# A graph layer and an expert layer in one kernel: the ranking of each group's expert choices is put a slot earlier, and its sums, places and sends with it

## The chip, the cores and the metric

The kernel runs on one NeuronCore of a Trainium2 chip. The metric is the time on the device in microseconds (us), the median of several runs. The core's engines each work through a queue of their own in order and wait for each other through semaphores: TensorE (PE; its weight loads are shown as PEld), VectorE (DVE), ScalarE (ACT), GpSimd (POOL) and SyncE (SP), which here only issues transfers. POOL issues the indirect transfers (gathers and scatters of rows by index).

## What is computed

There are 6250 nodes with 256 features and 100000 edges with 96 features, sorted by the node that they end in. All is float32.

```python
xn   = layernorm(x)
sum_, max_, mean_ = per node over its edges: sum, max (0 if none), sum / max(count, 1)
h    = relu(concat[xn, sum_, max_, mean_, u[0]] @ W1 + b1) @ W2 + b2      # 1024 hidden
x1   = x + h + xn
g    = layernorm(x1)
v, e = top_k(g @ gate_w + gate_b, 2)                                      # 2 of 16 experts
w    = softmax(v)
y    = g + sum over the two: w_k * (relu(g @ w1[e_k] + b1[e_k]) @ w2[e_k] + b2[e_k])
out  = x1 + layernorm(y) * gamma + beta
```

## The kernel before

**Tiles and groups.** The nodes are 50 tiles of 125. Thirteen groups of four tiles (group 0 has two) are worked from the last nodes to the first. The edges' sums and maxima come from two sources: groups 0 and 1 gather windows of edges; for all others an "edge stream" on DVE runs over seven regions of the edges (regions 0 to 6), loads chunks (`raw`), makes running sums and maxima (`rw`, lines 323 to 327), and stores them to `rows_d` through SP (line 336). At the end of a region its run sums are joined over partitions (`chain_runs`, lines 382 to 446, with two small transposes on PE), and a "carry" is stored to `carry_d` on POOL's queue (line 444). Groups then gather rows (`take_edges`, line 726) and carries (`take_carry`, line 733), and DVE joins them (`join_edges`, lines 739 and 741).

**Slots.** The order of the work is written out by hand: `at_slot(T, fn, ...)` puts a function into slot T, twelve slots to a group, and the list is sorted by slot and then by the order of entry (lines 1354 to 1371). Emitted in that order, each instruction joins the queue of its engine. Group g's matmuls stand in slots 12g to 12g+11: eight of `hidden` (line 775) and four of `output` (line 783, one per tile). What follows group g stands among group g+1's matmuls. Counted from slot 12(g+1): 0, the last `residual` (line 788); 1 to 3, `root_b`, `scale_b` and `norm_b` (line 811, ACT), which writes the normed rows twice into `xr`; 4 and 5, `turn_b` (line 820, PE); 6, `logits` (line 828, PE); 7, `choose` (lines 835 to 842: DVE takes the two best of 16 per row, ACT an exponential); 8, `rank`; 9, `rank_2`; 10, `place`; 11 and the slot after it, `send`, two tiles each. `xr` has one buffer, so the next group's `norm_b` must wait until the sends have read it.

**Ranking and sending.** `rank` (lines 848 to 855, DVE) turns the choices into a mask `mm` and adds it to running counts `M`, tile by tile. `rank_2` (lines 862 and 863, PE) multiplies by a triangular matrix and by ones, which sums over partitions and gives every row its number within its expert; it writes the PSUM tile `pg`, of which there is one, also used by `logits` and `bounds`. `place` (lines 871 to 884, DVE) turns that into row addresses in `xg_d` and writes the weights and the return addresses into `xr`. `send` (line 888, POOL) scatters 125 rows of 1032 bytes for each of a tile's two choices, with a small memset after each (line 893).

**The planner's credit.** Between two slots the loop gives the edge stream what is left of 4.6 us after the slot's own costs (`cost=` in `at_slot`). So a step that is put elsewhere also moves stream items. Small PE steps of the stream are held back to a slot's end (`for_pe`, `tell_pe`).

**Gathers between.** `take_blocks` (line 499) gathers blocks of dst on POOL's queue, in slots that fall among the places and sends of groups 1, 3 and 4; it is entered after them in the list, so within one slot it stands after them.

**Experts.** After the groups, `xg_d` is worked in blocks of 256 rows: `load_block` (lines 1025 to 1032, SP: two register loads, the rows `xb`, the 1 MB weights `wt`, the bias `eb`), `turn_block` (lines 1039 to 1050) for the next block in the middle of a block, `run_block` (lines 1061 to 1085: two matmul layers, and the results scattered by POOL to `y_d`). A block's load is issued three blocks ahead. The load reads `xg_d` at an address from a register, so it waits for all sends that were emitted before it, and sends wait for loads emitted before them. Blocks 0 to 13 are placed at slot 156 + 1.6b, so the steps that follow the last group (group 12, from slot 156) lie among them: `choose` in slot 163 stands after block 4 (162.4), slot 164's steps before block 5 (164.0), and so on. A last phase adds the two results of each node, norms and writes.

Of the kernel before, what the change touches and what calls it, by code (L numbers as in the profile page):

```python
# [35 lines left out]
SLOTS = 12  # L36
# [7 lines left out]
def kernel(  # L44
# [1047 lines left out]
    def at_slot(T, fn, *a, cost=0.0):  # L1092
        tasks.append((T, len(tasks), fn, a, cost))
# [15 lines left out]
    for g, (a, z) in enumerate(GRP):  # L1109
        B, n = SLOTS * g, z - a  # L1110
# [4 lines left out]
    for g, (a, z) in enumerate(GRP):  # L1115
        B, n = SLOTS * g, z - a
        if g:
            if g > 1:
                at_slot(max(0, B - 17), take_x, g)
                at_slot(B - 14, stats_x, g, 0, cost=1.2)  # L1120
                at_slot(B - 13, stats_x, g, 1, cost=1.2)
            if g > 1:
                at_slot(B - 11, root_x, g)
                at_slot(B - 10, scale_x, g, cost=0.5)
            at_slot(B - 9, norm_x, g)
            for i in range(n):
                if g >= GW:
                    late = 3 if g == GW else 0
                    at_slot(B - 10 + late + i // 2, take_edges, region[g], g, i)
                    at_slot(B - 9 + late + i // 2, take_carry, region[g], g, i)  # L1130
                else:
                    for h in range(2):
                        at_slot(2 * i + h, cut_window, g, i, h * WE // 2, (h + 1) * WE // 2, None)
                        at_slot(2 * i + 1 + h, sum_half, g, i, h)
                    at_slot(2 * i + 1, max_window, g, i, cost=4.7)
                    at_slot(2 * i + 2, add_window, g, i, cost=0.9)
                    at_slot(2 * i + 2, mask_window, g, i, cost=0.4)
                    at_slot(min(2 * i + 5, SLOTS - 2), mean_window, g, i)
            at_slot(B - 7, keep_x, g)
            for k in range(DC):  # L1140
                at_slot(B - 6 + k, turn, g, k)
            for i in range(n if g >= GW else 0):
                at_slot(B - (4 if g == GW else 6) + i // 2, join_edges, g, i, cost=0.6)
                at_slot(B - (4 if g == GW else 5) + i // 2, mask_edges, g, i)
            for k in range(DC, KC + 1):
                at_slot(B - 3 + k - DC + (1 if g == GW and k < DC + 2 else 0), turn, g, k)
        for i in range(n):
            at_slot(B + HC + 1 + i, residual, g, i, cost=1.1)
        early = GS - n
        at_slot(B + SLOTS + 1 - early, root_b, g)  # L1150
        at_slot(B + SLOTS + 2 - early, scale_b, g, cost=0.3)
        at_slot(B + SLOTS + 3, norm_b, g)
        for k in range(DC):
            at_slot(B + SLOTS + 4 + k, turn_b, g, k)
        at_slot(B + SLOTS + 6, logits, g)
        at_slot(B + SLOTS + 7, choose, g, cost=2.2)
        at_slot(B + SLOTS + 8, rank, g, cost=1.3)
        at_slot(B + SLOTS + 9, rank_2, g)
        at_slot(B + SLOTS + 10, place, g, cost=1.5)
        for i in range(n):  # L1160
            at_slot(B + SLOTS + 11 + i // 2, send, g, i)
    T = SLOTS * (NG - 3) + 21
    at_slot(T, open_experts)
    at_slot(T, count_full)
# [137 lines left out]
    with tc.manual_schedule():  # L1302
# [54 lines left out]
        for slot, _, fn, args, cost in tasks:  # L1357
            while slot > T:
# [6 lines left out]
                g = min(T // SLOTS, NG - 1)  # L1365
# [123 lines left out]
```

## Time and profile before

| | us |
|---|---|
| median of 3 runs | 1401.33 (1400.38 to 1401.83) |
| profiled execution, its own time | 1403.48 |
| its span | 1401.7 |
| PE busy in the span | 1195.1 |
| DVE busy in the span | 898.2 |
| granted TensorE clock, mean | 0.932 |

The profile's page lists busy time per engine over the span and in 40 equal slices of 35 us (a digit is tenths). Groups of instructions are named by line, engine, operation and tiles, output before inputs; each row of the timeline has start, duration, engine, line, operation, tiles, count, and in brackets the idle time of the engine just before it and what ended that. The name of what ended a wait is inferred from semaphores and can be a neighbour's. On PE each float32 matmul shows as two records, so an `output` of 8 matmuls shows as 16.

The rows at the places that the change touches, by group (us from the span's start):

| group | choose | rank | rank_2 on PE, wait before it | place | sends |
|---|---|---|---|---|---|
| 1 | 250.4 | 253.0 | 258.4, 0 | 262.7 | 273.9 to 287.0 |
| 3 | 369.9 | 374.3 | 375.1, 4.1 | 382.0 | 393.6 to 406.8 |
| 4 | 436.7 | 441.1 | 443.9, 0 | 450.1 | 462.5 to 478.2 |
| 9 | 740.4 | 744.3 | 745.1, 2.9 | 749.5 | 751.5 to 763.1 |
| 11 | 836.0 | 837.8 | 846.1, 0 | 846.7 | 849.5 to 861.1 |
| 12 | 906.1 | 907.9 | 914.4, 0 | 923.0 | 926.5 to 944.5 |

### The profile page before, as it was taken

The numbers are of one execution on the slowest core, as the hardware profiler recorded it, in microseconds if no ns is written. First come the engines' busy times: TensorE is split into PE (matmuls) and PEld (weight loads), VectorE is DVE, ScalarE is ACT, GpSimd is POOL, SyncE is SP. The second block draws the span as 40 slices with busy tenths as digits, with TensorE's granted clock in tenths as the row PEclk, the third lists the DMA queues.
The fourth block names the chain that finished last, engine by engine and source line by source line (L and its number), as shares of the span: only waits on it lengthen the run. The fifth ranks groups of instructions, "written<-read, shape, count | busy, mean of one in ns | idle before, by whom it ended". The sixth has DMA issues, their size and how long they took to land. (4 is left out here: it accounts for less than half of the span.)

```text
span 1401.7 us, 16643 instructions
## 1 busy us (share of the span) xinstructions
PE 1195.1 (85%) x4835; PEld 833.7 (59%) x4835; DVE 898.2 (64%) x2319; ACT 510.6 (36%) x1178; POOL 519.4 (37%) x611
## 2 busy tenths in 40 slices
PE   2598458979869789998898998899999999999683
PEld 1263244636626364564545647787888888888562
DVE  5477669969986989998777314343444455444277
ACT  3485135644528354353343532211212212121233
POOL 4133044563374736346253414152333333333100
PEclk9898779989989899999999999999999999999897
DMA  6953687796979897898985143457667786766396
GB/s 163 205 139 103 167 247 189 223 264 180 266 203 254 242 275 202 241 267 221 262 244 167 33 158 120 170 176 253 228 232 268 246 271 223 240 216 208 104 273 194
DMA packets 187240, 292.28 MB, mean 209 GB/s; under 512 B 35309, under 2 KB 153582, under 8 KB 179840
## 3 DMA queue, kind: packets, MB, share of 16 engines
q1 hardware_dynamic: 150800, 234.36, 56.5%
q0 software_dynamic: 36224, 56.33, 14.3%
q8 instruction: 41, 0.67, 0.2%
q14 instruction: 63, 0.52, 0.1%
q10 hardware_dynamic: 112, 0.41, 0.1%
HBM read 169.70 MB, written 123.21 MB: 209 GB/s over the span
## 5 line engine op out<-in xcount | busy, mean ns | idle before, releaser
L775 PE MATMUL acc<-inT,w1x 128*128 128x500 f32 (+1 forms) x832 | 378.7, 606 | 0.0
L775 PEld LDWEIGHTS acc<-inT,w1x 128*128 128x128 f32 x832 | 164.1, 205 | 184.8 <-issue 182.5
L1080 POOL DMA_INDIRECT y_d<-yb,to_i x114 | 133.1, 1168 | 296.6 <-ACT yb L1079 272.9
L1061 PE MATMUL acc<-xT,wt 128*128 128x256 f32 x912 | 223.1, 388 | 8.0 <-ACT hb L1067 6.2
L1074 PE MATMUL acc<-wt,hb 128*128 128x256 f32 x912 | 207.7, 380 | 6.5 <-DVE hb L1065 6.5
L888 POOL DMA_INDIRECT xg_d<-xr,pos_i x100 | 127.8, 1278 | 206.0 <-DVE xr L884 127.3
L783 PE MATMUL acc<-w2s,hT 128*125 128x256 f32 x800 | 187.9, 392 | 12.9 <-ACT hT L777 12.9
L1061 PEld LDWEIGHTS acc<-xT,wt 128*128 128x128 f32 x912 | 169.4, 191 | 39.8 <-ACT hb L1067 15.5
L1074 PEld LDWEIGHTS acc<-wt,hb 128*128 128x128 f32 x912 | 172.5, 190 | 32.4 <-DVE hb L1065 8.9
L1079 ACT ACTIVATE yb<-yb,xb 128x256 f32<-128x256 f32 x114 | 51.8, 501 | 348.1 <-issue 300.6
L783 PEld LDWEIGHTS acc<-w2s,hT 128*125 128x125 f32 x800 | 153.5, 196 | 37.2 <-ACT hT L777 13.3
L777 ACT ACTIVATE hT<-acc,c 128x500 f32<-128x500 f32 (+1 forms) x104 | 68.4, 658 | 225.2 <-PE acc L775 224.9
L1077 DVE TENSOR_TENSOR yb<-acc,xb 128x512 f32<-128x512 f32 x57 | 39.4, 691 | 162.8 <-PE acc L1074 162.8
L499 POOL DMA_INDIRECT gb<-in_dst_dram,blk_i x50 | 69.0, 1381 | 117.2 <-DVE blk_i L496 52.0
L323 DVE TENSOR_TENSOR rw<-rw,keep 125x768 f32<-125x768 f32 x81 | 76.9, 949 | 46.5 <-DMA rows_d<-rw 46.5
L1041 DVE COPY xT<-pT 128x512 f32<-128x512 f32 x57 | 39.3, 690 | 77.8 <-PE pT L1039 73.2
L324 DVE TENSOR_TENSOR rw<-rw,bar 125x768 f32<-125x768 f32 x81 | 84.7, 1046 | 0.0
L327 DVE TENSOR_TENSOR rw<-rw,raw 125x768 f32<-125x768 f32 x88 | 83.8, 952 | 0.0
L326 DVE TENSOR_TENSOR rw<-rw,raw 125x768 f32<-125x768 f32 x88 | 83.6, 950 | 0.0
L726 POOL DMA_INDIRECT at<-rows_d,first_i x44 | 64.4, 1464 | 35.0 <-issue 25.4
L760 ACT COPY inT<-pT 128x500 f32<-128x500 f32 (+1 forms) x65 | 35.9, 552 | 88.5 <-PE pT L759 81.7
L1408 PE MATMUL py<-yk,ident 125*125 125x256 f32 x200 | 52.2, 419 | 18.4 <-DMA yk<-y_d 18.1
(288 smaller groups left out, 1516.4 us busy)
## 6 DMA issues: line engine op xcount, KB each, us to landing
wt<-in_wpack_dram SPq DMA_DIRECT2D x57, 1026.0 KB
rows_d<-rw SPq DMA_DIRECT2D x46, 960.0 KB
rows_d<-rw SPq DMA_DIRECT2D x46, 540.0 KB
raw<-in_edge_dram SPq DMA_DIRECT2D x46, 480.0 KB
xb<-xg_d SPq DMA_DIRECT2D x57, 258.0 KB
raw<-in_edge_dram SPq DMA_DIRECT2D x46, 270.0 KB
eb<-in_eb_dram SPq DMA_DIRECT2D x57, 128.0 KB
xt<-in_x_dram SPq DMA_DIRECT2D x12, 500.0 KB
```

What stands on the lines that cost most here:

```text
L323: nc.vector.tensor_tensor(su, prev[0], keep[c][:, :, s + j, None].to_broadcast(bcast), op=OP.mult)
L324: nc.vector.tensor_tensor(mx, prev[1], bar[c][:, :, s + j, None].to_broadcast(bcast), op=OP.min)
L326: nc.vector.tensor_tensor(su, su, x_j, op=OP.add)
L327: nc.vector.tensor_tensor(mx, mx, x_j, op=OP.max)
L499: nc.gpsimd.indirect_dma_start(out=gbs_[t], out_offset=None, in_=dst_b, in_offset=IndirectOffsetOnAxis(ap=blk_i[:, t:t + 1], axis=0))
L775: nc.tensor.matmul(pH[:, :n * P], w1x[:, k, ms], inT[:, k, :n * P], start=False, stop=(k == KC - 1))
L777: nc.scalar.activation(h[:, :n * P], pH[:, :n * P], AF.Relu, bias=c1[:, m:m + 1])
L783: nc.tensor.matmul(pO, G[g]["hT"][m][:, i * P:(i + 1) * P], w2s[:, m, :], start=(m == 0), stop=(m == HC - 1))
L888: d = nc.gpsimd.indirect_dma_start(out=xg_d[:, :], out_offset=IndirectOffsetOnAxis(ap=G[g]["pos"][:, i, k:k + 1], axis=0), in_=G[g]["xr"][ ...
L1061: nc.tensor.matmul(pB[i][:, half, :], wt[:, k * FF + m * 128:k * FF + (m + 1) * 128], xT[:, k, :], start=(k == 0), stop=(k == DC - 1))
L1074: nc.tensor.matmul(pY[:, h, :], hb[:, m, h * 128:(h + 1) * 128], wt[:, W2O + m * D:W2O + (m + 1) * D], start=(m == order[0]), stop=(m == o ...
L1080: d = nc.gpsimd.indirect_dma_start(out=y_d[:, :], out_offset=IndirectOffsetOnAxis(ap=BL[b]["to"][:, h:h + 1], axis=0), in_=yb[:, h, :], in ...
```

## The change

`rank` goes from slot 8 to slot 7, right behind `choose` of the same group; `rank_2`, `place` and the sends each go one slot earlier, in all thirteen groups. No instruction is added or removed; tiles, buffers and costs stay as they are.

```diff
         at_slot(B + SLOTS + 6, logits, g)
         at_slot(B + SLOTS + 7, choose, g, cost=2.2)
-        at_slot(B + SLOTS + 8, rank, g, cost=1.3)
-        at_slot(B + SLOTS + 9, rank_2, g)
-        at_slot(B + SLOTS + 10, place, g, cost=1.5)
+        at_slot(B + SLOTS + 7, rank, g, cost=1.3)
+        at_slot(B + SLOTS + 8, rank_2, g)
+        at_slot(B + SLOTS + 9, place, g, cost=1.5)
         for i in range(n):
-            at_slot(B + SLOTS + 11 + i // 2, send, g, i)
+            at_slot(B + SLOTS + 10 + i // 2, send, g, i)
```

In the queues this means: on PE, `rank_2` stands before the next group's second output and not after it (for group 12, before block 5 and not after it); on DVE, `rank` stands before the second pair of `join_edges`, and `place` before the first `residual`; on POOL, the first four sends of groups 1, 3 and 4 stand before a `take_blocks` and not after it, and for group 12 all eight sends stand before block 7 and before block 10's load, where four stood after both.

## The prediction

> **What bounds the kernel now.** I read the busy rows by slice first, then stretches of the span, then PE's waits, then the order of time around them.
>
> ```profile
> PE 1195.1 (85%) x4835; PEld 833.7 (59%) x4835; DVE 898.2 (64%) x2319; ACT 510.6 (36%) x1178; POOL 519.4 (37%) x611
> PE   2598458979869789998898998899999999999683
> DVE  5477669969986989998777314343444455444277
> DMA  6953687796979897898985143457667786766396
> ```
>
> A slice is 35 us. To about 745 us (slice 21) DVE and the DMA engines are as full as PE; from there to 1305 PE alone is. The stretches say the same:
>
> ```profile
> 255.00:275.00 20.00, 19.34 (x88) 13.71 (x87) 19.28 (x46) 11.20 (x33) 7.14 (x6) 1.00 0.59 168
> 275.00:300.00 25.00, 14.86 (x41) 6.17 (x40) 21.36 (x42) 9.63 (x19) 21.13 (x24) 0.85 0.92 244
> 420.00:745.00 325.00, 293.69 (x1062) 172.09 (x1062) 278.33 (x677) 148.88 (x314) 156.20 (x146) 0.93 0.88 246
> 750.00:890.00 140.00, 132.81 (x559) 89.66 (x558) 47.61 (x179) 47.04 (x85) 49.99 (x71) 1.00 0.37 117
> 960.00:1305.00 345.00, 343.01 (x1624) 292.26 (x1623) 156.02 (x327) 74.16 (x183) 115.62 (x181) 1.00 0.69 232
> ```
>
> Columns: stretch, its length, busy time of PE, its weight loads, DVE, ACT, POOL, then granted clock, DMA share, GB/s. Up to 745 us what decides is whichever of DVE and PE last waited for the other; after it every idle microsecond of PE counts in full.
>
> **Part 1: the sends leave POOL's queue sooner (groups 1, 3, 4).** In group 1 `place` ends at 264.4, yet its sends start at 273.9: four gathers of dst blocks (slot 34, L499) stand before them, and those wait until 267.2 for their indices.
>
> ```profile
> 267.22 1.24 POOL L499 DMA_INDIRECT gb<-in_dst_dram,blk_i  x1 [5.29 <-DVE blk_i L496]
> 273.94 1.43 POOL L888 DMA_INDIRECT xg_d<-xr,pos_i  x1 [0.30 <-issue]
> 285.56 1.43 POOL L888 DMA_INDIRECT xg_d<-xr,pos_i  x1 [0.21 <-issue]
> ```
>
> ```profile
> 295.75 2.93 ACT L811 ACTIVATE xr<-xt,stat 125x512 f32<-125x512 f32 x4 [12.46 <-DMA gb<-in_dst_dram,blk_i]
> ```
>
> ```profile
> 307.47 0.32 DVE L739 SCALAR_TENSOR_TENSOR at<-cg,cross,at 125x96 f32<-125x96 f32 x1 [8.88 <-DMA cg<-carry_d,next_i]
> ```
>
> `xr` has one buffer, so ACT's next norm waits for the last send to land (issued 285.6, landed about 295.6, though the row names a gather), and PE's turn at 296.6 waits 9.4 us with it; the carry gathers behind the sends hold DVE 8.9 us. After the change `place` follows the run sums directly and ends near 259.9; four sends fit between 260 and 266, before the gathers. Carry store 2 (0.6 us) moves behind the gathers, so the last four sends run 274.5 to 281.4 instead of ending at 287.0: **-5.6 us**, and the later gathers, ACT's norm and DVE's join come as much sooner. DVE reaches that join at 298.6, so 8.9 us of wait can give 5.6. Eight transfers and eight small memsets move; their count is unchanged. Here the Trainium skill speaks against the change: DMA: Bandwidth & Descriptors, section Issuing engines are not separate DMA queues, says that transfers from any engine share the same 16 engines, so an earlier issue buys no bandwidth. By the rule alone the gain is 0 if DMA limits; the row of 255 to 275 has DMA at 0.59, that is 8 us free, and four sends are about 0.5 MB, some 2 us at the 244 GB/s of the next row. I take -5.6 (bounds -6.5, 0). Groups 3 and 4 have the same queue (sends 393.6 to 406.8 behind gathers at 387.0; 462.5 to 478.2 behind 456.4), and PE waits for `xr` 12.8 and 4.9 us. But DVE stands at 429.7 for 13.3 us on a row store on SP's queue, not on `xr`, so a sooner PE only waits for DVE: 0 (bounds -8, 0, see the first rival).
>
> **Part 2: PE's sum over partitions (rank_2).** `rank` costs the same 1.6 us on DVE; it loses the join and stream work between it and `choose`. But rank_2 stands one output (3.6 us) sooner in PE's queue, and behind it wait output 1, the turns and the next group. In groups 3 to 9 PE already waits there:
>
> ```profile
> 735.14 7.07 PE L783 MATMUL acc<-w2s,hT 128*125 128x256 f32 x32
> 745.08 0.43 PE L862 MATMUL pg<-mm,before 125*125 125x64 f32 x2 [2.86 <-DVE mm L853]
> 747.00 5.09 PE L783 MATMUL acc<-w2s,hT 128*125 128x256 f32 x16
> ```
>
> In groups 3 to 8 (rank_2 from the end of `choose` + 1.9 us, then one output of 3.5 us) PE comes 0.1 to 2.9 us later, 4.6 in group 3 where the planner puts two more stream items ahead. DVE takes the residuals 2.6 to 12.8 us after PE has them, so this is hidden: 0 (bounds 0, +2); without that slack it is some 9 us. Group 0: +3.1, hidden by PE's wait of 5.1 us at 201.6. Group 9 is PE's last wait for DVE before the PE-bound part. `choose` ends at 742.2; unshifted, rank_2 ends 744.1 and the output 747.6 against 746.1, +1.5; by the planner's credit DVE has 1.9 us less ahead of it, -0.4. I take **+0.5** (bounds -0.4, +3). Groups 10 and 11: DVE waits for PE, sums are ready 5 us early: 0. The carry stores of regions 3 and 6 slip two slots and one: about 11 and 3.6 us on POOL, whose readers have that slack (joins at 365.5; DVE idle 7.7 us before 786.2): 0 (bounds 0, +4).
>
> **Part 3: the last group.** Slots are now expert blocks. Before, block 5 lay between `choose` and rank_2.
>
> ```profile
> 901.85 3.62 PE L1074 MATMUL acc<-wt,hb 128*128 128x256 f32 x16
> 905.31 1.89 PE L1061 MATMUL acc<-xT,wt 128*128 128x256 f32 x8
> 909.12 1.99 PE L1061 MATMUL acc<-xT,wt 128*128 128x256 f32 x8 [1.49 <-ACT hb L1067]
> ```
>
> After, rank_2 follows block 4 at once: PE idles from 905.5 to 908.7 (`mm` ends 908.67), rank_2 ends about 909.5, block 5 takes 7.6 and ends 917.1; block 6 began at 914.8 before: **+2.3 us**. The clock adds to it:
>
> ```profile
> 374.00:382.00 8.00, 6.88 (x22) 5.70 (x23) 7.73 (x17) 4.77 (x15) 0.00 (x0) 0.57 0.78 207
> 893.00:900.00 7.00, 7.00 (x26) 6.18 (x27) 0.00 (x0) 0.95 (x2) 1.48 (x4) 0.52 0.53 208
> ```
>
> The first followed a PE wait of 4.1 us, the second one of 1.7 us among small matmuls. The skill's TensorE: Matmul & The Clock Gate, section HAM oscillation, sets the limit at idle gaps of about 3.4 us: by it a gap of 3.2 costs nothing more; by the rows half clock follows for about 6 us, **+3.0** (bounds 0, +3.4). I take the rows.
>
> **Part 4: the last sends and the blocks' loads.** Before, four sends stood ahead of block 10's load and four ahead of block 11's; now all eight stand before block 10's, whose first transfer waits for them on SP with the weights and bias behind it.
>
> ```profile
> 943.28 1.18 POOL L888 DMA_INDIRECT xg_d<-xr,pos_i  x1 [0.21 <-issue]
> ```
>
> ```profile
> 947.45 0.31 SPq L1028 DMA_DIRECT2D xb<-xg_d  x1
> ```
>
> ```profile
> 955.04 0.69 DVE L1044 TENSOR_TENSOR xb<-xb,eb 128x512 f32<-128x512 f32 x1 [3.46 <-DMA eb<-in_eb_dram]
> ```
>
> The load goes 2.8 us after the last send ends; the bias lands 7.0 us after the weights are issued (948.0). The sends stay behind block 6's own scatters: 928.8 + 7 x 1.48 + 1.2 = 940.3, load at 943.5 (935.4 before), weights 944.1, bias 951.1. Block 9 then waits: DVE 951.1, PE 952.3, its end about 955.8 against 948.1. Block 10 no longer waits (2.8 us before) and ends 963.4 against 959.1: +4.3, of which 2.3 is part 3's: **+2.0**, and +1.5 for the clock over two PE waits of 4 and 3 us (bounds of both together 0, +7).
>
> **Sum.** -5.6 + 0 + 0.5 + 2.3 + 3.0 + 2.0 + 1.5 = **+3.7 us**. The profiled execution took 1403.48 us (span 1401.7 and 1.8 around it): 1407.2 there, span 1405.4; the runs' median lies 2.15 below it, so **1405.0 us** against 1401.33.
>
> **Rivals.** Faster: in group 3 the early sends fill the DMA hole of 388 to 394 us and are gone when SP comes to the row store that DVE then waits for. That store kept SP for 10.0 us (407.3 to 417.3), where the pieces beside it took 0.6 to 2.4; at 2 us DVE gains 8: 1405.0 - 8 = 1397.0. From 0.9 us on the kernel is not slower by the bound below, from 6.5 on it is faster. For it: DVE's 13.3 us wait at 429.7, DMA at 0.85 while those sends run. Against: the sends are only 4 of some 20 transfers on POOL's queue there. Clearly slower: the front gain is swallowed by the next row-store wait: 1405.0 + 5.6 = 1410.6; for it DMA at 0.88 from 420 to 745, against it nothing there is tied to a fixed time. Cancelled: no clock loss (-4.5): 1400.5.
>
> **How the numbers follow.** Forecast 0.50 (own range 1401 to 1409, a quarter of it inside the bound), faster rival 0.25, clearly slower 0.12, cancelled 0.13. A measurement of this kernel can tell 0.2%, 2.8 us: slower 0.38 + 0.12 + 0.01 = 0.51, same 0.12 + 0.10 = 0.22, faster 0.25 + 0.02 = 0.27. The range, 1393.5 to 1411, leaves about one in ten at each end.
>
> **What would show it.** Sends of group 1 on both sides of the four gathers; ACT's wait near 12.5 down to 7; DVE's wait for cg from 8.9 to 3; PE waiting about 3.2 us for mm between blocks 4 and 5, a half clock after it; the load of block 10 waiting for eight sends and block 9 standing on its bias. The prediction is wrong if DVE's later store waits change by more than some 5 us, or if the granted clock stays at 1.00 from 906 to 960.

## The result and the profile after

The changed kernel takes 1417.56 us (median of 4 runs, 1415.83 to 1419.93); the kernel before took 1400.86 us (1398.83 to 1401.83) beside it. The ratio is 1.0122, 95% interval 1.0103 to 1.0141: slower by 17 us, where 4 were predicted. The time lies outside the range of the prediction.

The busy rows of the page after, and its rows by slice:

```profile
PE 1204.4 (85%) x4835; PEld 837.6 (59%) x4835; DVE 901.4 (64%) x2319; ACT 512.1 (36%) x1178; POOL 533.3 (38%) x611
...
PE   2598459998898769898989998889999999999683
...
DVE  5477669986987789889887414343444444534277
...
DMA  5954676797879688988896243446677877766395
```

No engine has more instructions, and DVE has 3 us more of busy time in 14 us more of span. To see where the span grew I used `choose` (L835), which each group runs once on DVE, as a milestone:

| choose of group | before, us | after, us | difference |
|---|---|---|---|
| 0 | 188.3 | 187.7 | -0.6 |
| 1 | 250.4 | 254.1 | +3.7 |
| 2 | 311.9 | 308.9 | -3.0 |
| 3 | 369.9 | 380.1 | +10.2 |
| 4 | 436.7 | 441.7 | +5.0 |
| 6 | 568.8 | 577.1 | +8.3 |
| 9 | 740.4 | 750.2 | +9.8 |
| 12 | 906.1 | 913.1 | +7.0 |
| end of span | 1401.7 | 1415.8 | +14.1 |

So there are two losses. One builds up over the groups, with ups and downs: some 4 us by group 1, 10 by group 3 (where DVE has done one piece of edge work more than before: nine between choose of groups 2 and 3, not eight), 5 at group 4, and again nearly 10 at group 9; 7.0 are left at group 12. The other, 7.1 us, comes after the last `choose`. (Some of the expectations below split the 14.1 us as 9 and 5; the table gives 7.0 and 7.1.) Between choose of group 1 and of group 2 there is a gain of 6.7 us, at the place that part 1 of the prediction named.

**The first loss is idle time of DVE.** The stretch from choose of group 0 to choose of group 9 (columns as in the prediction: stretch, length, busy time of PE, its weight loads, DVE, ACT, POOL, then clock, DMA share, GB/s), before:

```profile
188.30:740.40 552.10, 484.11 (x1769) 286.19 (x1768) 476.39 (x1209) 253.26 (x546) 274.45 (x259) 0.92 0.85 236
```

and after:

```profile
187.70:750.20 562.50, 492.54 (x1759) 290.22 (x1760) 476.25 (x1206) 253.86 (x546) 286.20 (x259) 0.91 0.83 232
```

DVE does the same work, 476.4 and 476.25 us. The stretch is 10.4 us longer, and all of it is time in which DVE stands. What it stands for, in the view of its waits in that stretch (us in total, times, longest), before:

```profile
DVE rw L323 <- DMA rows_d<-rw: 34.8, 6, 13.3
DVE at L739 <- DMA cg<-carry_d,next_i: 12.6, 3, 8.9
DVE stat L803 <- ACT stat L798: 6.1, 4, 2.2
DVE bsa L690 <- DMA xt<-in_x_dram: 5.5, 6, 2.8
```

and after:

```profile
DVE bsa L690 <- DMA xt<-in_x_dram: 28.9, 7, 8.7
DVE at L739 <- DMA cg<-carry_d,next_i: 12.3, 6, 3.6
DVE rw L323 <- DMA rows_d<-rw: 9.2, 3, 3.3
DVE bsa L690 <- issue: 8.3, 1, 8.3
```

The waits for row stores did shrink, by 22 us with one of 3.3 that is put down to "issue". In their place DVE now stands 37.2 us (28.9 + 8.3) at L690, the first statistics of a group's x, because the load of x (`take_x`, L680, on SP's queue) has not landed. Before it was 5.5. The largest of these waits that the view puts down to the load, in the order of time after:

```profile
464.35 0.43 DVE L690 BATCH_NORM_STATS2 bsa<-xt 125x6 f32<-125x256 f32 x1 [8.65 <-DMA xt<-in_x_dram]
```

and SP's queue ahead of that load, after:

```profile
441.80 2.43 SPq L183 DMA_DIRECT2D raw<-in_edge_dram  x2
444.28 2.56 SPq L336 DMA_DIRECT2D rows_d<-rw  x2
446.95 1.71 SPq L680 DMA_DIRECT2D xt<-in_x_dram  x1
```

The same place before:

```profile
428.27 5.44 SPq L183 DMA_DIRECT2D raw<-in_edge_dram  x2
433.76 2.76 SPq L336 DMA_DIRECT2D rows_d<-rw  x2
436.61 1.85 SPq L680 DMA_DIRECT2D xt<-in_x_dram  x1
```

`take_x` of a group has the slot in which `choose` of the group three before it stands, so both can be measured from that choose. Over groups 3 to 11 before, SP issued the load 2.0 us after choose on average and DVE came to L690 15.6 us after choose. After, SP issues it 4.7 us after choose and DVE comes at 14.6. In the five groups in which DVE then waits more than 3 us, x takes 11 to 17 us from issue to use, 14 on average (the load is 500 KB). The 13.6 us that lay between before (15.6 - 2.0) held no slack; the 9.9 us after are 4 too few. In the program's order one piece of edge work more (a load and a row store) stands ahead of the loads of groups 6 and 7 on SP: 19 and 24 stores instead of 18 and 23. These two groups have 12.6 of the 37.2 us (4.0 and 8.7). For the other groups up to 11 SP's order is that of before: no piece passes their loads, but the same transfers are posted later after choose, or DVE comes to L690 sooner. In group 5, with the wait of 8.3 us, choose came 3.0 us sooner than before and the load 3.3 us later (316.6 against 313.3); a few transfers ahead of it one pair of edge loads held SP for 11.6 us (284.5 to 296.1). What held it there was not tried.

**The signs of part 1 are there.** ACT's norm, PE's turn behind it, and DVE's join in group 1:

```profile
295.09 2.93 ACT L811 ACTIVATE xr<-xt,stat 125x512 f32<-125x512 f32 x4 [4.87 <-DMA gb<-in_dst_dram,blk_i]
...
295.96 0.33 PE L820 MATMUL pT<-ident,xr 125*128 125x125 f32 x1 [1.85 <-ACT xr L811]
...
305.85 0.32 DVE L739 SCALAR_TENSOR_TENSOR at<-cg,cross,at 125x96 f32<-125x96 f32 x1
```

ACT waits 4.87 us instead of 12.46, PE 1.85 instead of 9.44, and DVE's join, which waited 8.88 us, does not wait at all. POOL issues four sends (263.9 to 269.7) ahead of the gathers of dst blocks at 271.3, and the others behind carry store 2, from 279.1:

```profile
263.93 1.22 POOL L888 DMA_INDIRECT xg_d<-xr,pos_i  x1 [5.67 <-DVE xr L884]
...
278.23 0.61 POOL L444 DMA_DIRECT2D carry_d<-ct  x1
...
284.10 1.43 POOL L888 DMA_INDIRECT xg_d<-xr,pos_i  x1 [0.21 <-DMA raw<-in_edge_dram]
```

The last send ends 31.4 us after choose of group 1 (36.6 before).

**The second loss**, at the last group: PE's wait for `mm` between blocks 4 and 5, and its wait in the middle of block 9.

```profile
915.82 0.40 PE L862 MATMUL pg<-mm,before 125*125 125x64 f32 x2 [3.36 <-DVE mm L853]
916.35 0.68 PE L863 MATMUL pg<-M,ones 125*125 125x64 f32 x2
916.83 3.41 PE L1061 MATMUL acc<-xT,wt 128*128 128x256 f32 x8
920.08 0.60 PE L1039 MATMUL pT<-ident,xb 128*128 128x128 f32 x4
920.51 1.89 PE L1061 MATMUL acc<-xT,wt 128*128 128x256 f32 x8
...
955.75 1.08 PE L1039 MATMUL pT<-ident,xb 128*128 128x128 f32 x4 [5.00 <-DMA xb<-xg_d]
956.63 3.62 PE L1061 MATMUL acc<-xT,wt 128*128 128x256 f32 x8
```

The granted clock (third number from the right) behind these two waits:

```profile
915.00:925.00 10.00, 9.05 (x37) 7.79 (x38) 3.54 (x12) 1.64 (x4) 1.18 (x4) 0.83 0.35 132
...
953.00:960.00 7.00, 4.25 (x12) 3.60 (x13) 1.84 (x9) 0.00 (x0) 2.07 (x4) 0.57 0.88 265
```

### The profile page after: what moved, and what is told of

Same layout as the page of the kernel before. It is cut to its first block, busy times and chain, and to the rows that moved or that the text cites. A ratio compares the mean times of both kernels' runs of the same rounds, so it can differ in the third digit from the quotient of the medians.

```text
span 1415.8 us, 16630 instructions
## 1 busy us (share of the span) xinstructions
PE 1204.4 (85%) x4835; PEld 837.6 (59%) x4835; DVE 901.4 (64%) x2319; ACT 512.1 (36%) x1178; POOL 533.3 (38%) x611
## 5 line engine op out<-in xcount | busy, mean ns | idle before, releaser
L1074 PE MATMUL acc<-wt,hb 128*128 128x256 f32 x912 | 207.8, 380 | 2.9 <-DVE hb L1065 2.9
L783 PE MATMUL acc<-w2s,hT 128*125 128x256 f32 x800 | 194.0, 399 | 13.0 <-ACT hT L777 13.0
L1074 PEld LDWEIGHTS acc<-wt,hb 128*128 128x128 f32 x912 | 173.0, 190 | 28.7 <-DVE hb L1065 4.9
L323 DVE TENSOR_TENSOR rw<-rw,keep 125x768 f32<-125x768 f32 x81 | 80.0, 987 | 24.1 <-DMA rows_d<-rw 20.8
L327 DVE TENSOR_TENSOR rw<-rw,raw 125x768 f32<-125x768 f32 x88 | 88.9, 1011 | 0.0
L726 POOL DMA_INDIRECT at<-rows_d,first_i x44 | 70.9, 1612 | 34.2 <-PE acc L775 12.5
L326 DVE TENSOR_TENSOR rw<-rw,raw 125x768 f32<-125x768 f32 x88 | 83.8, 952 | 0.0
L324 DVE TENSOR_TENSOR rw<-rw,bar 125x768 f32<-125x768 f32 x81 | 77.2, 954 | 0.0
L770 PE MATMUL acc<-inT,w1r 32*128 32x500 f32 (+1 forms) x208 | 45.5, 673 | 33.6 <-DVE xt L788 25.8
L733 POOL DMA_INDIRECT cg<-carry_d,next_i x44 | 60.6, 1377 | 24.9 <-issue 11.5
```

The lines of the kernel that those rows point to most:

```text
L323: nc.vector.tensor_tensor(su, prev[0], keep[c][:, :, s + j, None].to_broadcast(bcast), op=OP.mult)
L324: nc.vector.tensor_tensor(mx, prev[1], bar[c][:, :, s + j, None].to_broadcast(bcast), op=OP.min)
L326: nc.vector.tensor_tensor(su, su, x_j, op=OP.add)
L327: nc.vector.tensor_tensor(mx, mx, x_j, op=OP.max)
L726: nc.gpsimd.indirect_dma_start(out=G[g]["at"][:, i, 0:2 * EF], out_offset=None, in_=rows_d[0:EP * sum(JR[:c + 1]), :], in_offset=IndirectO ...
L783: nc.tensor.matmul(pO, G[g]["hT"][m][:, i * P:(i + 1) * P], w2s[:, m, :], start=(m == 0), stop=(m == HC - 1))
```

## Experiments

The first theory after the result, **X**: the pieces of edge work that the planner hands out have moved against the load of x, and DVE stands for x. Its rival **P**: PE meets rank_2 sooner in its queue, waits there (31.5 us in six rows against 9.8 in four in the stretch above), and DVE's waits only fill time that it would have stood elsewhere. Single executions scatter by some 10 us in these comparisons, so the verdicts rest on the ratios to the kernel before and their intervals; the rows show mechanisms. All diffs are against the changed kernel or, where it says so, against the kernel before.

**The load of x two slots sooner.** The same instructions in the same order on PE, DVE, ACT and POOL; SP alone differs.

```
-                at_slot(max(0, B - 17), take_x, g)
+                at_slot(max(0, B - 19), take_x, g)
```

> The changed kernel with one more edit: the load of a group's x is issued two slots sooner. Theory X (DVE now reaches the first statistics of x before x has landed: 37.2 us of waits in eight rows against 7.7 before): those waits fall below 8 us, and the 9 us lost before the last group's choose come back: about 1408.5. Theory P (PE, which waits for mm earlier in its queue, sets the pace, and DVE's waits for x only take up time that DVE would have stood elsewhere): the waits for x vanish, others grow by as much, 1415 to 1418.

Measured 1402.89 us, ratio 1.0007 (0.9987 to 1.0027), against 1.0122 for the changed kernel. An earlier place for the load of x, on SP alone, gives nearly the whole loss back. DVE's waits for x are gone; the longest that are left in the same stretch:

```profile
DVE at L739 <- DMA cg<-carry_d,next_i: 28.5, 7, 7.6
DVE rw L323 <- DMA rows_d<-rw: 21.1, 7, 5.8
DVE lg L835 <- PE pg L828: 5.3, 1, 5.3
```

PE waits longer for `mm` than in the changed kernel, in a kernel that is 15 us faster. In the same stretch of the kernel before, of the changed one and of this one:

```profile
PE pg L862 <- DVE mm L853: 9.8, 4, 4.1
PE pg L862 <- DVE mm L853: 31.5, 6, 10.7
PE pg L862 <- DVE mm L853: 42.7, 6, 15.8
```

That speaks against P; it is more than theory X asked for, since the loss behind the last choose is still in this kernel.

The control, the same edit in the kernel before:

> The kernel before with the load of x two slots sooner, as a control. Its waits for x are 7.7 us in seven rows. Theory X: at most part of that comes back, 1396 to 1400. Theory P: no change, 1400 to 1402. If moving one load of 0.5 MB disturbs the row stores of the same queue: 1403 or more.

Measured 1398.48 us, ratio 0.9993 (0.9977 to 1.0010). The sooner load by itself is worth nothing that can be told. What it mends in the changed kernel, the change brought.

**Rank alone.** rank in the slot of choose with its cost; rank_2, place and sends in the slots of before.

```
-        at_slot(B + SLOTS + 8, rank_2, g)
-        at_slot(B + SLOTS + 9, place, g, cost=1.5)
+        at_slot(B + SLOTS + 9, rank_2, g)
+        at_slot(B + SLOTS + 10, place, g, cost=1.5)
...
-            at_slot(B + SLOTS + 10 + i // 2, send, g, i)
+            at_slot(B + SLOTS + 11 + i // 2, send, g, i)
```

> Only rank goes to the slot of choose; rank_2, place and the sends keep their slots. PE's order against its own work is that of before. Theory P: nothing is lost, 1399 to 1402. Theory X: rank leaves the stretch between the load of x and its statistics, so about half of the added waits for x are there, and half of the 9 us is lost: 1404 to 1408.

Measured 1416.3 us, ratio 1.0122 (1.0075 to 1.0168). With rank_2 in its old slot everything is lost all the same: P falls. X has missed too. Its account gave half the loss, and in this profile the waits for x are small, while those for the carries (`cg`) are 40.1 us in the stretch where they were 12.6:

```profile
DVE at L739 <- DMA cg<-carry_d,next_i: 40.1, 9, 13.2
DVE bsa L690 <- DMA xt<-in_x_dram: 12.6, 5, 3.5
```

**What of rank does it: its place on DVE, or its credit?** A step's cost is taken from the slot's time, and what is left is filled with pieces of edge work. So two kernels, both against the kernel before, each with one half. Credit alone:

```
-        at_slot(B + SLOTS + 8, rank, g, cost=1.3)
-        at_slot(B + SLOTS + 9, rank_2, g)
+        at_slot(B + SLOTS + 8, rank, g, cost=0.0)
+        at_slot(B + SLOTS + 9, rank_2, g); at_slot(B + SLOTS + 7, lambda: None, cost=1.3)
```

> Nothing of rank is moved; only its 1.3 us of planner's credit is charged one slot sooner, so that the same pieces of edge work are handed out in other slots (SP's order of transfers is then exactly that of the changed kernel). Rank moved with its credit cost 1.2% (1416.3 against 1399.8). Theory S (the shift of the edge pieces against the loads, joins and statistics does the harm): as much here, 1412 to 1418. Theory O (it is rank's own place on DVE, ahead of the pieces of its slot): no change, 1398 to 1402.

Place alone:

```
-        at_slot(B + SLOTS + 8, rank, g, cost=1.3)
-        at_slot(B + SLOTS + 9, rank_2, g)
+        at_slot(B + SLOTS + 7, rank, g, cost=0.0)
+        at_slot(B + SLOTS + 9, rank_2, g); at_slot(B + SLOTS + 8, lambda: None, cost=1.3)
```

> Rank stands directly behind choose, but its credit is charged in the old slot: PE, ACT, POOL and SP keep the order of before, only DVE's differs. Theory S: no change, 1398 to 1402. Theory O: 1412 to 1418.

Credit alone: 1418.5 us, ratio 1.0150 (1.0116 to 1.0184). Place alone: 1399.65 us, ratio 1.0001 (0.9981 to 1.0022). This is the cleanest pair of the study. Not one step of the routing is moved in the first, and it is as slow as the changed kernel; rank stands directly behind choose in the second, and nothing is lost. Theory S holds, theory O falls: **1.3 us of bookkeeping, charged one slot sooner, costs about 20 us** (16 to 26 by the interval).

**The whole change with the credit left where it was.**

```
-        at_slot(B + SLOTS + 7, rank, g, cost=1.3)
-        at_slot(B + SLOTS + 8, rank_2, g)
-        at_slot(B + SLOTS + 9, place, g, cost=1.5)
+        at_slot(B + SLOTS + 7, rank, g, cost=0.0)
+        at_slot(B + SLOTS + 8, rank_2, g); at_slot(B + SLOTS + 8, lambda: None, cost=1.3); at_slot(B + SLOTS + 10, lambda: None, cost=1.5)
+        at_slot(B + SLOTS + 9, place, g, cost=0.0)
```

> The whole change with the credit of rank and place charged in the old slots (SP's order is that of before). Theory S: the waits for x fall back to some 8 us and the 14 to 17 us of loss shrink to the steps of the prediction, -5.6 in group 1 and +5 behind the last group: 1398 to 1406. Theory O: 1413 to 1419.

Measured 1402.74 us, ratio 1.0013 (0.9990 to 1.0037). This is close to the kernel that the prediction worked out: +1.8 us (-1.4 to +5.2) where its sum says +3.7. One thing differs: carry store 2 keeps its place ahead of group 1's sends, and the prediction had moved it behind them. The shift of the pieces is then the difference between 1.0122 and 1.0013, about 15 us.

**Is the late x all of the shift?** The kernel with the credit alone, with the edit of `take_x` to B - 19 on top of it.

> The shift of credit alone cost 1.5% (1418.5), with only 16.0 us of waits for x in its profile but 37.5 us for the carries (cg). If the late load of x is the whole cause, the sooner load gives everything back: 1398 to 1402. If the pieces' new places delay the carry gathers by themselves, only the waits for x come back: 1405 to 1412.

Measured 1409.81 us, ratio 1.0076 (1.0051 to 1.0102). Half comes back; the rest is at the carries, as the second expectation had it. DVE at its longest wait, and POOL ahead of the gather that ends it:

```profile
511.69 0.32 DVE L739 SCALAR_TENSOR_TENSOR at<-cg,cross,at 125x96 f32<-125x96 f32 x1 [15.56 <-DMA cg<-carry_d,next_i]
...
481.37 1.91 POOL L888 DMA_INDIRECT xg_d<-xr,pos_i  x1 [0.22 <-issue]
483.30 0.61 POOL L444 DMA_DIRECT2D carry_d<-ct  x1
488.42 8.83 POOL L726 DMA_INDIRECT at<-rows_d,first_i  x1 [4.51 <-issue]
...
505.08 1.20 POOL L733 DMA_INDIRECT cg<-carry_d,next_i  x1 [0.30 <-issue]
```

Eight sends in their old slots end at 483.3; behind them stand the carry store, two gathers of edge rows, of which the first is held until 497.3, four gathers of dst blocks, and only then the carries. DVE is at the join at 496.1. In the changed kernel the sends stand a slot sooner in this queue, and with the sooner x it takes 1402.89, not 1409.81, although it has the last group's loss as well. So with the pieces in their new places the sooner steps are worth more than with the pieces in the old ones. Which of the steps does it, and why the gather at 488.4 was held, was not tried.

**Group 1 alone**, with the credit in the old slots: meant as the first part of the prediction by itself.

```
-        at_slot(B + SLOTS + 7, rank, g, cost=1.3)
-        at_slot(B + SLOTS + 8, rank_2, g)
-        at_slot(B + SLOTS + 9, place, g, cost=1.5)
+        late = int(g != 1)
+        at_slot(B + SLOTS + 7 + late, rank, g)
+        at_slot(B + SLOTS + 8 + late, rank_2, g); at_slot(B + SLOTS + 8, lambda: None, cost=1.3); at_slot(B + SLOTS + 10, lambda: None, cost=1.5)
+        at_slot(B + SLOTS + 9 + late, place, g)
...
-            at_slot(B + SLOTS + 10 + i // 2, send, g, i)
+            at_slot(B + SLOTS + 10 + late + i // 2, send, g, i)
```

> The change in group 1 alone, with all credit in the old slots: the sends of group 1 leave ahead of the four gathers, nothing else. The prediction's first part: -5.6 (bounds -6.5 to 0), about 1394. If the gain is eaten by DVE's later waits for row stores and carries: 1399 to 1400.

Measured 1395.83 us, ratio 0.9978 (0.9959 to 0.9997): -3.1 us (-5.7 to -0.4). A gain, a little over half of the term. But it is a weaker form of part 1: with the credit in its old slots, carry store 2 still stands ahead of the sends, and they wait with it for `ct`.

```profile
262.13 0.58 POOL L444 DMA_DIRECT2D carry_d<-ct  x1 [8.50 <-DVE ct L442]
263.01 1.67 POOL L888 DMA_INDIRECT xg_d<-xr,pos_i  x1 [0.30 <-issue]
...
282.00 1.18 POOL L888 DMA_INDIRECT xg_d<-xr,pos_i  x1 [0.22 <-issue]
```

The last send ends 33.7 us after choose of group 1 (249.5 here), 2.9 sooner than before and not 5.2, and choose of group 2 comes 2.7 us sooner after it (58.8 us against 61.5), in line with the time.

**The last group in its old slots**, the others changed.

```
-        at_slot(B + SLOTS + 7, rank, g, cost=1.3)
-        at_slot(B + SLOTS + 8, rank_2, g)
-        at_slot(B + SLOTS + 9, place, g, cost=1.5)
+        late = int(g == NG - 1)
+        at_slot(B + SLOTS + 7 + late, rank, g, cost=1.3)
+        at_slot(B + SLOTS + 8 + late, rank_2, g)
+        at_slot(B + SLOTS + 9 + late, place, g, cost=1.5)
...
-            at_slot(B + SLOTS + 10 + i // 2, send, g, i)
+            at_slot(B + SLOTS + 10 + late + i // 2, send, g, i)
```

> The change for groups 0 to 11; the last group keeps its old slots. Of the 14.1 us that the changed kernel's span is longer, 9 are there by the last group's choose and 5 come after it. If those 5 are the price of the last group's own steps (rank_2 between blocks 4 and 5, all eight sends ahead of block 10's load): 5 us below the changed kernel, about 1412.5. If they are a late echo of what happened before 906 us (the blocks' loads standing behind other transfers): no gain, about 1417.5.

Measured 1412.75 us, ratio 1.0082 (1.0050 to 1.0113). By itself its interval still touches that of the changed kernel. With the load of x sooner as well (both edits together) it is clear:

> The change for groups 0 to 11, the last group in its old slots, and the load of x two slots sooner. The changed kernel with the sooner load alone took 1402.9. If the last group's steps cost 5 us by themselves: about 1398. If that price was not there any more: 1402 to 1403.

Measured 1394.12 us, ratio 0.9956 (0.9939 to 0.9973), against 1.0007 (0.9987 to 1.0027) with the last group new: the last group's steps cost 7 us, give or take some 4, and **this kernel beats the one before by 6 us**. To split the 7, only the last group's sends go back, rank_2 stays between the blocks. Against the changed kernel with x sooner:

```
-            at_slot(B + SLOTS + 10 + i // 2, send, g, i)
+            at_slot(B + SLOTS + (11 if g == NG - 1 else 10) + i // 2, send, g, i)
```

> The changed kernel with the sooner load of x, and the last group's eight sends in their old slots (half before block 10's load, half after it); its rank_2 stays between blocks 4 and 5. All-new took 1402.9, all-old of the last group 1394.1. By the prediction's terms rank_2 with its clock is 5.3 of 8.8 and the sends 3.5: 1399.4. By the marks of the trace (block 5 ends 4.3 us later after the last choose, the end 7.1 us later): 1398.4 to 1400.0. If the load behind eight sends is the whole price: 1394 to 1395.

Measured 1400.98 us, ratio 1.0021 (1.0001 to 1.0040): nothing comes back. The marks of the trace say why. The end of a block's last matmul (L1074, sixteen a block) after the last choose, us (one execution each; over all traces the end of the span comes 494.0 to 499.8 after it in the ten kernels with the last rank_2 in its old slot, and 500.7 to 503.0 in the four with it early):

| kernel | block 5 | block 9 | block 10 | end of span |
|---|---|---|---|---|
| before | 8.5 | 41.4 | 53.0 | 495.6 |
| changed | 12.8 | 52.4 | 60.5 | 502.7 |
| x sooner | 12.8 | 51.6 | 59.8 | 500.8 |
| x sooner, last sends old | 12.8 | 45.7 | 59.2 | 500.7 |
| x sooner, last group old | 8.5 | 43.0 | 52.8 | 495.1 |

With the sends back, block 10's load goes sooner, but block 11's then waits for the second four: PE's one wait of 5.4 us becomes two of 2.2 and 3.0. In both kernels the first send is issued 25.0 us after the last choose, before it was 20.4. So what is left as the cause is rank_2 between blocks 4 and 5: it sets block 5 back by 4.3 us, and the sends start 4.6 us later. That is a cause by elimination; no kernel moves the last rank_2 by itself.

**All three**: groups 0 to 11 new with the credit in the old slots, the last group old, x sooner (the edits shown for group 1, with `late` as for the last group, and the one for `take_x`).

> The change in groups 0 to 11 with the credit in the old slots, the last group old, the load of x two slots sooner. With the credit shifted the same took 1394.1. If the shift of the edge pieces does harm only by the late load of x: 1393 to 1396. If it also delays the carries: lower, 1388 to 1391.

Measured 1392.12 us, ratio 0.9956 (0.9938 to 0.9973): the same ratio as with the credit shifted, and between the two expected ranges. Once x is early and the sends are sooner, no harm of the shift can be told.

## Why the prediction was wrong

**The step that failed** is part 2 with its "this is hidden: 0 (bounds 0, +2)" for groups 3 to 8. It followed rank_2 through PE's queue and measured DVE's slack towards PE. That much held: with the credit left in its old slots the whole change costs 1.8 us. It used the planner's credit for single places (two stream items in group 3, "DVE has 1.9 us less ahead of it" in group 9, the carry stores), and gave no term to what the pieces of edge work that are pushed out of a slot do to the loads of x. Each piece is a load and a store on SP, the queue that posts x too, and DVE work ahead of the statistics of x. That the loads of x had no slack could be read from the trace of before: issue at +2.0 from choose, need at +15.6, about 14 us from issue to use (9.7 to 17.3 in the nine groups), and seven small waits at L690. The runs put +15 us in the place of 0 (1.0122 against 1.0013). In the changed kernel the late x is enough to account for it, since the sooner load gives it back; with the credit alone half of the loss is at the carries, and how it gets there stays open.

**Part 1** was right: its order on POOL and its waits came as described, and in the queue its size too. In the five traces with carry store 2 behind the gathers the last send of group 1 ends 5.2 to 5.6 us sooner after choose (5.6 predicted). What choose of group 2 keeps of it differs, 2.7 to 6.7 us, and this form was not timed by itself; the weaker one, group 1 alone, gives -3.1. The rule weighed there from the Trainium skill (DMA: Bandwidth & Descriptors, Issuing engines are not separate DMA queues) would make the gain 0 if DMA limits. From 255 to 275 us the DMA share was 0.62 in the changed kernel (0.59 before), so it did not limit, and the interval of group 1 alone excludes 0, narrowly: what was gained is a place in a queue, not bandwidth.

**Carry stores** (part 2, "0 (bounds 0, +4)"): the steps alone do not move them, the credit does. The store of region 3 leaves 26.7 us after choose of group 2 before, 26.2 with the credit left in place, 38.3 with the credit alone (about the 11 us later that the prediction gives) and 47.4 in the changed kernel, which has both. With the credit alone DVE's waits for carries are 47.8 us in the whole span, against 21.3 before, so the 0 is in doubt; which of these waits come from the slip was not separated.

**Parts 3 and 4**, 8.8 us together, were nearly right in their sum: 7.1 us by the marks (502.7 - 495.6) and 7 us by the two timed kernels. That is in part luck, since several of their terms were off. The clock after PE's wait of 3.36 us: eight matmuls took 3.41 us and eight of the same row 1.89 soon after, 1.5 us lost instead of 3.0; the granted clock of 0.83 over 10 us is half clock for some 3.4 us, not 6. That lies between the rule of the skill's TensorE: Matmul & The Clock Gate, HAM oscillation (nothing below some 3.4 us) and the rows of before that I took. And the sends start 25.0 us after choose, not 22.7, because block 6's scatters wait for ACT. So block 10's load is issued at 953.1, 3.1 us after the last send ends (the prediction said 2.8; its own lines give 3.0). PE then stands in the middle of block 9 for 5.0 us, at the turns of block 10, which wait for its `xb`; the prediction had it wait for that load's bias, which costs PE only 1.2 us more. And the +2.0 of part 4, for eight sends ahead of block 10's load, has no support: with four of them put back, nothing came back.

**The rivals.** The clearly slower one, a front gain swallowed by the next wait, was nearest, though it named a row store and 5.6 us. Of the faster one a part was seen: DVE's store waits shrank by 22 us, and the kernel with x sooner and the last group old is 6 us faster than before. Its mechanism, group 3's early sends in a hole of DMA, was not tested. In the changed kernel the added waits for x (32 us) are more than these 22. The prediction's own warning, store waits changed by more than 5 us, is the one that came true.

## To carry to other kernels

Where a planner fills slots with work from a stream, a step's cost entry is an instruction too: before moving it, list which stream items move, which queues they post on, and what stands behind them there. For every load that the bound engine will wait for, work out issue, landing and need from one common milestone; a slack near zero, shown by small waits in many rows, is the place where a shift of 2 to 4 us turns into a wait in nearly every group. And split a "move" into its order and its bookkeeping: here one half cost nothing and the other about 20 us.

## What the hardware showed unexpectedly

A load of 500 KB took 11 to 17 us from issue to use with a DMA share of 0.83. At the 232 GB/s of that stretch its bytes are some 2 us, so most of that time is not its own; what else was in flight was not told apart. And after a PE wait of 3.36 us the next eight matmuls ran at about half speed for 3.4 us (granted clock 0.83 from 915 to 925), and then at full speed at once; after the wait of 5.00 us the half clock lasted some 6 of the 7 us from 953 on (0.57).
